# More copied tiles in a two-layer graph network: a second table, a third engine for its columns, and a narrower one-hot

## The chip, the core and the metric

The kernel runs on one core of a Trainium2 chip. A core has TensorE (PE), VectorE (DVE), ScalarE (ACT), GpSimd (POOL) and SyncE (SP), each with an instruction queue of its own that it works through in order; semaphores tie them together. The metric is the device time of one execution in microseconds, as the median of several runs. The lower the better.

## The reference

12,500 nodes have 128 features each, and 200,000 edges, sorted by their target `dst`, have 50 features each. Both layers add to `x` what they compute of its normalized form:

```python
h = relu(layernorm(x))
x = x + segment_sum(h[src], dst) @ W_rel.T + b_rel + h @ W_root.T
h = relu(layernorm(x))
w = silu(edge_attr_50 @ We1 + be1) @ We2 + be2
agg = segment_sum(h[src] * w, dst)
x = x + silu(agg @ Wn1 + bn1) @ Wn2 + bn2
```

All of it is f32.

## The kernel before

**Groups.** The edges are cut into tiles of 128 and groups of 8 tiles (`GT`), 196 groups a layer, the last with 3 tiles. Group g of both layers does the same: POOL gathers the source rows of a tile from DRAM into one of six buffers `hs` (`fetch`, line 250: one indirect DMA for a tile of 128 rows). DVE compares the targets with a row of numbers and so makes a one-hot `oh` of `W` = 128 nodes for each edge (`compare`, line 263). PE multiplies the rows with the one-hot, 8 matmuls into one PSUM window of 128 columns (`scatter`, line 376); since the edges are sorted, a group's targets lie in a window of few nodes. DVE adds the window to the sums in SBUF, `agg`, at an offset read from a register (`add`, line 394). In the second layer, PE and ACT make the edge weights for the group (`hidden`, `weigh`, lines 340, 343 and 353), and DVE adds the bias and multiplies (lines 361 and 365) ahead of the scatter.

**Copied tiles.** All of the normalized nodes lie transposed in SBUF, in `table`: a node is a column of 128 numbers. Some tiles are therefore not gathered by POOL, but put together from this table: the 128 source columns are copied one by one into a tile `hc`, at offsets that the engine reads into registers from a list, 16 at a time (`take`); DVE copies by an OR with zero on bytes (line 585), ACT by a copy (line 587). PE turns the tile (`turn`, line 612) and ACT places it into the last slot of its group's `hs` (`place`, line 618). `HELP` tells how many tiles are copied in how many groups, `HC` which columns of each tile DVE copies and which ACT. With `HELP = ((1, 1), (9, 10))`, one tile a group is copied in the first layer from group 30 on, and nine tiles in ten groups in the second from group 26 on: 160 + 147 tiles, each placed four groups (`HW`) after its copying. POOL issues the other 2819 gathers.

**First groups.** The table and the normalized nodes in DRAM, `h0_d`, are made beside the first groups of the first layer: `node_first` normalizes one batch of 512 nodes a group, stores it, turns it on PE, and ACT copies it into the table (line 449). Until group `FG` = 29 the groups gather from the raw `x`, and each tile is normalized after the gather (`norm`, two units a group). `push` runs a unit's second half after the first half of the next one. From FG on they gather from `h0_d`.

**Node steps.** When the last edge of a batch of 512 nodes is surely added, its node step runs: in the first layer `node_sum` (PE sums, DVE adds `x` and starts the statistics, ACT takes the deviation, DVE clears that part of `agg`), `node_norm`, `node_keep` and `node_store`, over four groups. The result h1 goes to DRAM, where the second layer gathers. For the second layer's table, each batch of h1 is loaded again from DRAM (`node_again`), turned and copied into `table` (`node_turn`) beside its first 26 groups.

**Order of the work.** It is written out by hand. The loop over groups records, for group g: the gathers of g + 1, the compare of g + 1, the add of g - 1, the scatter of g, then whatever `plan` has put beside g, then `spread`, which records this group's share of the column copies on DVE and ACT. `at` records a wait, `inc` an increment. Each engine's queue has this order and nothing else.

Of the kernel before, what the change touches and what calls it, by code (L numbers as in the profile page):

```python
# [10 lines left out]
F32 = mybir.dt.float32  # L11
# [12 lines left out]
W = 128  # L24
# [10 lines left out]
HELP = ((1, 1), (9, 10))  # L35
HC = (60, 56)
# [30 lines left out]
def helped(n_nodes, n_edges):  # L67

    ng = n_edges // GE
    nbt = len(last_groups(n_nodes, n_edges))
    layers = []
    for begin, (tiles, groups) in ((min(ng, nbt + FB) + 1, HELP[0]), (nbt + 1, HELP[1])):
        ends = (begin - 1 - -(i + 1) * groups // tiles for i in range(ng * tiles // groups))
        layers.append((begin, [(e + HW, e) for e in ends if e + HW < ng - 1]))
    return layers

# [12 lines left out]
def kernel(  # L92
# [41 lines left out]
    FG = min(NG, NBT + FB)  # L134
    helps = [
        (layer, h, e, begin, j)
        for layer, (begin, groups) in enumerate(helped(N, n_edges))
        for j, (h, e) in enumerate(groups)
    ]
    helped_groups = {(layer, h) for layer, h, *_ in helps}  # L140
# [17 lines left out]
    table = single([P, -(-N // P) * P], "table")  # L158
    agg = single([P, NW * WG], "agg")
    keep = table.rearrange("p (t d) -> p t d", d=D)  # L160
    table_b = table.bitcast(U8)
# [15 lines left out]
    with (  # L177
# [13 lines left out]
        hid = many(2, [P, GT * P], "hid")  # L191
        st, mv = many(2, [P, NB, 6], "st"), many(2, [P, NB, 2], "mv")
# [6 lines left out]
        help_i, = many(1, list(help_t.shape), "help_i", I32)  # L199
# [41 lines left out]
        def fetch(layer, g):  # L241
# [7 lines left out]
            for t in range(tiles_of[g] - ((layer, g) in helped_groups)):  # L249
                ins = G.indirect_dma_start(  # L250
                    out=hs[k % HB][:, t, :], out_offset=None,
                    in_=h1_d if layer else x if g < FG else h0_d,
                    in_offset=bass.IndirectOffsetOnAxis(
                        ap=src_sb[:, g * GT + t : g * GT + t + 1], axis=0
                    ),
                )
                done["hs", k] = inc(ins, f"hs{k % HB}", 16)
# [12 lines left out]
        def stats(xr, n, rows, st_, mv_, sd_, free):  # L270
# [7 lines left out]
            at(A, inc(ins, "dve"))  # L278
# [3 lines left out]
        def scales(n, rows, mv_, sd_, rs_, nm_, deviations):  # L282
            at(V, deviations)
# [50 lines left out]
        def hidden(g):  # L334
            n = tiles_of[g] * P
            at(T, done["ef", g // EG], done.get(("hid", g - 1)), done["const"])
            e = ef[g // EG % 2][:EF, g % EG * GE : (g % EG + 1) * GE]
# [4 lines left out]
            at(A, done["hp", g], done.get(("wp", g - 2)))  # L342
# [41 lines left out]
        def add(layer, g):  # L384
# [7 lines left out]
            at(V, done["ap", k], done.get(("add", k - 1)), done["agg"])  # L392
            window = agg[:, ds(firsts[k - g % GL][g % GL], W)]
# [51 lines left out]
        def node_table(b, turned):  # L445
# [3 lines left out]
            ins = A.copy(table[:, n0 : n0 + m], turned.rearrange("p t d -> p (t d)")[:, :m])  # L449
            done["table", b] = inc(ins, "act")  # L450

        def node_sum(b):

            n0, nt = batches[b]
            at(T, done.get(("keep", b - 1)), done["const"], done["ones"], done["table", b])
            T.matmul(op[:, :nt, :], ones_r, b_rel_r[:, :nt, :], start=True, stop=False)
            for layer_agg, w_sb in ((table, w_root_sb), (agg, w_rel_sb)):
                for t in range(nt):
                    s = n0 + t * P
                    ins = T.matmul(  # L460
                        op[:, t, :], layer_agg[:, s : s + P], w_sb,
                        start=False, stop=(layer_agg is agg and t == nt - 1),
                    )
                at(T, done["add", ready[b]])
            done["op", b] = inc(ins, "pe")
            at(V, done["op", b], done["xt", b])
            o = op[:, :nt, :]
            ins = V.tensor_add(o, o, xt[b % XB][:, :nt, :])  # L468
            done["dev", b] = stats(
                op, nt, P, stn[2], mvn[2], sdn[2], (inc(ins, "dve"), done.get(("h1", b - 1)))  # L470
            )
            ins = V.memset(agg[:, n0 : n0 + nt * P], 0.0)
            done["agg"] = inc(ins, "dve")

        def node_norm(b):
            n0, nt = batches[b]
            at(A, scales(nt, P, mvn[2], sdn[2], rsn[2], nmn[2], done["dev", b]))
            if b < 2:
                at(A, *(done["h0 out", b] for b in range(max(0, NBT - 3), NBT)))
            else:  # L480
                at(A, done["h1 out", b - 2], done["keep", b - 2])
# [20 lines left out]

        def node_again(b):

            i = b % 3
            at(S, done["h1 out", b], done.get(("turned again", b - 3)))
            if b < 3:
                at(S, *(done["h1 out", c] for c in range(max(0, NBT - 2), NBT)))
            done["h1 in", b] = node_dma(b, h0[i], h1_d, f"h1in{i}", True)

        def node_turn(b):

            n0, nt = batches[b]
            at(T, done["h1 in", b], done["b3"])
            for t in range(nt):
                ins = T.transpose(op[:, t, :], h0[b % 3][:, t, :], ident)  # L516
            done["turned", b] = done["turned again", b] = inc(ins, "pe")
            at(A, done["op", NBT - 1], *done.get("columns", ()))
            node_table(b, op)
            done["b3"] = done["table", b]  # L520

        def node_hidden(b):
# [3 lines left out]
            ins = T.matmul(b3[:, :m], wn1_sb, agg[:, n0 : n0 + m], start=True, stop=True)  # L526
# [31 lines left out]
        def chunks(layer, g, engine):  # L558

            first, last = (0, HC[layer]) if engine is V else (HC[layer], P)  # L560
# [5 lines left out]
        def take(engine, chunk):  # L566
# [3 lines left out]
            kind = mybir.EngineType.DVE if engine is V else mybir.EngineType.Activation  # L570
            _, places = nc.values_load_multi_w_load_instructions(  # L571
                help_at[i % P : i % P + 1, i // P, lo:hi], engines=[kind],
                min_val=TABLE, max_val=TABLE + 4 * (N - 1),
                skip_runtime_bounds_check_because="sources are nodes",
            )
            return chunk, places

        def put(engine, taken):

            (i, lo, hi), places = taken  # L580
            at(engine, done.get(("tile", i - 3)), *(done["table", b] for b in range(NBT)))
            for c, place_ in zip(range(lo, hi), places):
                to, column = hc_b[i % 3][:, 4 * c : 4 * c + 4], table_b[:, ds(place_ - TABLE, 4)]
# [6 lines left out]

        def spread(layer, g):
# [4 lines left out]
            for engine, rest in ((V, hooks), (A, list(chunks(layer, g, A)))):  # L596
                for chunk in rest or (chunks(layer, g, V) if engine is V and not layer else ()):
                    put(engine, take(engine, chunk))
            hooks.clear()

# [13 lines left out]
        def place(i, layer, h):  # L614
# [3 lines left out]
            done["hx", k] = done["placed", i] = inc(A.copy(hs[k % HB][:, GT - 1, :], bank), "act")  # L618
# [3 lines left out]
        with tc.tile_critical():  # L622
# [32 lines left out]
            done["agg"] = inc(A.copy(agg, zero.to_broadcast([P, NW * WG])), "act")  # L655
# [9 lines left out]
            ins = V.tensor_scalar(help_at, help_i, 4.0, float(TABLE), op0=ALU.mult, op1=ALU.add)  # L665
# [42 lines left out]

            for layer, parts in (
                (0, (node_sum, node_norm, node_keep, node_store)),  # L710
                (1, (node_hidden, node_out, node_out_store)),
            ):
                begin = 0 if layer else FG
                for b in range(NBT):
                    begin = max(begin, ready[b] + 1)
                    for i, part in enumerate(parts):
                        plan(layer, begin + i, lambda b=b, part=part: part(b))
                    begin += len(parts) - 1
            for b in range(min(XB, NBT)):
                plan(0, NBT + 1, lambda b=b: node_load(b))  # L720
            for b in range(NBT):
                plan(1, b - 1, lambda b=b: node_again(b))
                plan(1, b, lambda b=b: node_turn(b))
            for b in range(min(2, NBT)):
                plan(1, ready[0] - 1, lambda b=b: node_load(b, keep_d))
            for i, (layer, h, e, begin, j) in enumerate(helps):
# [6 lines left out]
                if not layer:  # L733
                    plan(0, e + 2, lambda i=i, h=h: place(i, 0, h))
# [240 lines left out]
```

## Time and profile before

| | |
|---|---|
| median of 3 runs | 3561.74 us (3557.4 to 3564.12) |
| the profiled execution | 3553.55 us, its span 3551.7 us |
| POOL busy | 2662.7 us (75%), 2819 gathers |
| ACT busy | 2620.0 us (74%), 21464 column copies |
| DVE busy | 2510.7 us (71%), 17832 column copies |
| PE busy | 2286.8 us (64%), weight loads 1833.0 us |
| first gather starts | 3.06 us |
| last gather ends | 3533.43 us |
| granted TensorE clock, mean | 0.753 |

How to read it: a row of the costliest groups names the line, the engine, the operation and its tiles, then the count, the busy time and the mean of one in ns, and behind the bar how long the engine sat idle just before such instructions and what ended most of that. "issue" is idle time in which the engine waited for nothing that the profile shows. A timeline row gives start and length in us. An f32 matmul stands as two records, each with a weight load (PEld).

### The profile page before, as it was taken

The numbers are of one execution on the slowest core, as the hardware profiler recorded it, in microseconds if no ns is written. First come the engines' busy times: TensorE is split into PE (matmuls) and PEld (weight loads), VectorE is DVE, ScalarE is ACT, GpSimd is POOL, SyncE is SP. The second block draws the span as 40 slices with busy tenths as digits, with TensorE's granted clock in tenths as the row PEclk, the third lists the DMA queues.
The fourth block names the chain that finished last, engine by engine and source line by source line (L and its number), as shares of the span: only waits on it lengthen the run. The fifth ranks groups of instructions, "written<-read, shape, count | busy, mean of one in ns | idle before, by whom it ended". The sixth has DMA issues, their size and how long they took to land.

```text
span 3551.7 us, 73201 instructions
## 1 busy us (share of the span) xinstructions
PE 2286.8 (64%) x11405; PEld 1833.0 (52%) x11405; DVE 2510.7 (71%) x20197; ACT 2620.0 (74%) x22584; POOL 2662.7 (75%) x2826
## 2 busy tenths in 40 slices
PE   3444455445454454455567778878888788888887
PEld 3443444444444444444456566656566566566565
DVE  5555777676766767776433378888888888888885
ACT  6554888788878878887511278987888789888984
POOL 7777777777777777777677777777777777777776
PEclk7566656666666667656678888898888888988988
DMA  4332322222222222222233333332332233333322
GB/s 123 106 96 74 83 69 63 63 66 69 63 63 68 66 63 66 69 61 60 84 105 105 95 82 86 88 85 79 87 89 83 81 87 90 84 83 86 87 82 62
DMA packets 201107, 284.08 MB, mean 80 GB/s; under 512 B 49305, under 2 KB 150260, under 8 KB 195620
## 3 DMA queue, kind: packets, MB, share of 16 engines
q0 software_dynamic: 90208, 184.93, 20.0%
q1 hardware_dynamic: 110214, 94.30, 8.7%
q14 instruction: 396, 3.24, 0.3%
q8 instruction: 93, 1.52, 0.2%
q10 hardware_dynamic: 196, 0.09, 0.0%
HBM read 253.52 MB, written 25.60 MB: 79 GB/s over the span
## 4 chain that ended last, share of the span: by engine, by line
POOL 59%; issue 20%; PE 9%; DVE 5%; DMA 5%; ACT 2%; DVEq 0%; ACTq 0%; POOLq 0%; SPq 0%
POOL hs L250 59%; DMA hs<-h_d,src_sb 5%; PE bank L376 4%; PE pair L353 2%; ACT hc L587 2%; DVE hc L585 2%; DVE hs L365 2%; PE pair L340 1%; DVE pair L361 1%; PE bank L460 0%; DVE oh L263 0%; PE bank L526 0%; DVEq L571 0%; DVE xt L545 0%; ACTq L571 0%
## 5 line engine op out<-in xcount | busy, mean ns | idle before, releaser
L250 POOL DMA_INDIRECT hs<-h_d,src_sb x2587 | 2442.5, 944 | 798.5 <-issue 776.6
L587 ACT COPY hc<-table 128x4 uint8 x21464 | 2135.3, 190 | 63.3 <-issue 52.1
L376 PE MATMUL bank<-oh,hs 128*128 128x128 f32 x6252 | 1214.2, 373 | 671.7 <-DVE hs L365 300.2
L376 PEld LDWEIGHTS bank<-oh,hs 128*128 128x128 f32 x6252 | 1127.2, 279 | 885.1 <-DVE hs L365 435.4
L585 DVE TENSOR_TENSOR hc<-table,bank 128x4 uint8<-128x4 uint8 x17832 | 1303.1, 150 | 282.6 <-issue 274.7
L263 DVE TENSOR_TENSOR oh<-bank,rel 128x1024 f32<-128x1024 f32 x392 | 475.0, 1212 | 0.1
L353 PE MATMUL pair<-we_sb,hid 128*128 128x128 f32 x3126 | 428.7, 296 | 3.4 <-DVE xt L488 3.4
L361 DVE TENSOR_TENSOR pair<-pair,be_sb 128x1024 f32<-128x1024 f32 x196 | 240.2, 1226 | 261.1 <-PE pair L353 260.8
L353 PEld LDWEIGHTS pair<-we_sb,hid 128*128 128x128 f32 x3126 | 418.5, 215 | 3.5 <-DVE xt L488 3.5
L340 PE MATMUL pair<-ef,we_sb 50*128 50x512 f32 (+1 forms) x782 | 409.3, 645 | 1.2 <-ACT hid L343 1.2
L365 DVE TENSOR_TENSOR hs<-pair,hs 128x1024 f32<-128x1024 f32 x196 | 239.4, 1221 | 163.5 <-DMA hs<-h_d,src_sb 151.8
L612 PE MATMUL pair<-ident,hc 128*128 128x128 f32 x160 | 64.1, 401 | 434.6 <-ACT hc L587 277.2
L343 ACT ACTIVATE hid<-pair,be_sb 128x1024 f32<-128x1024 f32 x196 | 216.9, 1107 | 106.8 <-PE pair L340 106.3
L250 POOL DMA_INDIRECT hs<-in_x,src_sb x232 | 219.0, 944 | 71.2 <-issue 70.4
L612 PEld LDWEIGHTS pair<-ident,hc 128*128 128x128 f32 x160 | 28.7, 180 | 460.1 <-issue 141.1
L340 PEld LDWEIGHTS pair<-ef,we_sb 50*128 50x128 f32 x782 | 135.0, 192 | 132.7 <-issue 120.2
L279 ACT ACTIVATE sdn<-mvn,eps 128x4 f32<-128x4 f32 (+1 forms) x50 | 14.5, 289 | 247.0 <-DVE mvn L277 247.0
L449 ACT COPY table<-bank 128x512 f32<-128x512 f32 (+1 forms) x25 | 14.4, 577 | 176.2 <-PE bank L516 176.2
L528 ACT ACTIVATE hid<-bank,bn_sb 128x512 f32<-128x512 f32 (+1 forms) x25 | 17.0, 678 | 153.9 <-PE bank L526 153.9
L274 DVE BATCH_NORM_STATS2 st<-hs 128x6 f32<-128x128 f32 x232 | 50.3, 279 | 111.2 <-DMA hs<-in_x,src_sb 111.2
L394 DVE TENSOR_TENSOR agg<-agg,bank 128x128 f32 x392 | 109.2, 279 | 27.0 <-PE bank L376 19.7
L468 DVE TENSOR_TENSOR bank<-bank,xt 128x512 f32<-128x512 f32 (+1 forms) x25 | 17.2, 688 | 149.4 <-PE bank L460 149.4
(68 smaller groups left out, 910.4 us busy)
## 6 DMA issues: line engine op xcount, KB each, us to landing
hs<-h_d,src_sb POOLq DMA_INDIRECT x2587
ef<-in_ef_t SPq DMA_DIRECT2D x98, 408.0 KB
xt<-in_x SPq DMA_DIRECT2D x48, 256.0 KB, 3.9
h_d<-h SPq DMA_DIRECT2D x48, 256.0 KB, 2.5
keep_d<-xt SPq DMA_DIRECT2D x24, 256.0 KB, 2.4
h<-h_d SPq DMA_DIRECT2D x24, 256.0 KB, 5.3
xt<-keep_d SPq DMA_DIRECT2D x24, 256.0 KB, 10.0
out_x<-xt SPq DMA_DIRECT2D x24, 256.0 KB, 2.7
```

Of the source, the lines that this page charges most:

```text
L250: ins = G.indirect_dma_start(out=hs[k % HB][:, t, :], out_offset=None, in_=h1_d if layer else x if g < FG else h0_d, in_offset=bass.Indire ...
L263: return V.tensor_tensor(oh[k % OB][:, :n, :], io.unsqueeze(1).to_broadcast([P, n, W]), rel[:, g, :n].unsqueeze(2).to_broadcast([P, n, W]) ...
L340: ins = T.matmul(hp_b[:, c : c + m], we1_sb, e[:, c : c + m], start=True, stop=True)
L343: ins = A.activation(hid[g % 2][:, :n], hp_b[:, :n], AF.Silu, bias=be1_sb)
L353: ins = T.matmul(wp[:, t, :], hid[g % 2][:, t * P : (t + 1) * P], we2_sb, start=True, stop=True)
L361: ins = V.tensor_add(w, w, be2_sb.unsqueeze(1).to_broadcast([P, n, D]))
L365: done["msg", g] = inc(V.tensor_mul(h, w, h), "dve")
L376: ins = T.matmul(ap[k % AB], hs[k % HB][:, t, :], oh[k % OB][:, t, :], start=(t == 0), stop=(t == tiles_of[g] - 1),)
L394: done["add", k] = inc(V.tensor_add(window, window, ap[k % AB]), "dve")
L585: ins = V.tensor_tensor(to, column, zero_b, ALU.bitwise_or)
L587: ins = A.copy(to, column)
L612: done["tile", i] = inc(T.transpose(bank, hc[i % 3], ident), "pe")
```

## The change

- **Copied tiles.** `HELP` becomes six tiles in five groups of the first layer and nineteen in twenty groups of the second. Where two tiles fall into one group, a `slot` tells them apart. They begin at group 18 in the first layer and at group 1 in the second: 206 + 179 tiles.
- **A third engine.** In the first layer, the last 12 of a tile's 128 columns are moved by PE: a matmul of the identity with one column of the table, into PSUM (`move`); in the next group ACT copies the piece into `hc` (`empty`). DVE copies columns 0 to 55 and ACT 56 to 115 in the first layer; 0 to 59 and 60 to 127 in the second. In the first layer one list of DVE's is now read ahead, after the compare (`hook`).
- **Tables sooner.** Two batches of nodes are normalized a group instead of one, so `FG` is 17 instead of 29.
- **Two tables.** `table` and `agg` become the two halves of one tile `both`. The first layer's table is the first half and its sums are the second; in the second layer it is the other way round. The second layer's table is made in the node step of the first: `node_turn` turns h1 from SBUF, and `node_send` copies it over the sums just used. `node_again`, with its loads from DRAM, is gone. The old table is cleared for the new sums by four copies on ACT (`clear`) beside groups 191 to 194, its last two batches by DVE.
- **Node steps.** The parts of a node step lie a group apart, over seven groups, and closer together in the last ones.
- **One-hot.** `W` is 80 instead of 128.

Cut to its core:

```diff
-W = 128
+W = 80
...
-HELP = ((1, 1), (9, 10))
-HC = (60, 56)
+HELP = ((6, 5), (19, 20))
+HC = ((56, 116), (60, 128))
...
-    for begin, (tiles, groups) in ((min(ng, nbt + FB) + 1, HELP[0]), (nbt + 1, HELP[1])):
-        ends = (begin - 1 - -(i + 1) * groups // tiles for i in range(ng * tiles // groups))
-        layers.append((begin, [(e + HW, e) for e in ends if e + HW < ng - 1]))
+    for begin, (tiles, groups) in ((min(ng, -(-nbt // 2) + FB) + 1, HELP[0]), (1, HELP[1])):
+        ends = [begin - 1 - -(i + 1) * groups // tiles for i in range(ng * tiles // groups)]
+        slots = [ends[:i].count(e) for i, e in enumerate(ends)]
+        layers.append((begin, [(e + HW, s, e) for s, e in zip(slots, ends) if e + HW < ng - 1]))
     return layers
+def help_places(n_nodes, n_edges):
+    places, begins, begin = [], [], 0
+    for _, groups in helped(n_nodes, n_edges):
+        begins.append(begin)
+        places += [(j % P, begin + j // P) for j in range(len(groups))]
+        begin += -(-max(len(groups), 1) // P)
+    return places, begins + [begin]
...
-    FG = min(NG, NBT + FB)
+    FG = min(NG, -(-NBT // 2) + FB)
...
-    table = single([P, -(-N // P) * P], "table")
-    agg = single([P, NW * WG], "agg")
-    keep = table.rearrange("p (t d) -> p t d", d=D)
-    table_b = table.bitcast(U8)
+    both = single([P, 2 * NW * WG], "both")
+    halves = both[:, : NW * WG], both[:, NW * WG :]
+    agg = halves[1]
+    keep = halves[0].rearrange("p (t d) -> p t d", d=D)
+    both_b = both.bitcast(U8)
...
-            for t in range(tiles_of[g] - ((layer, g) in helped_groups)):
+            for t in range(tiles_of[g] - helped_groups.count((layer, g))):
...
         def hidden(g):
...
+            if g < 2:
+                at(T, done.get(("emptied", done.get("moved"))))
...
-            window = agg[:, ds(firsts[k - g % GL][g % GL], W)]
+            window = halves[1 - layer][:, ds(firsts[k - g % GL][g % GL], W)]
...
-            at(T, done.get(("keep", b - 1)), done["const"], done["ones"], done["table", b])
+            at(T, done.get(("sent", b - 1)), done["const"], done["ones"], done["table", b])
             T.matmul(op[:, :nt, :], ones_r, b_rel_r[:, :nt, :], start=True, stop=False)
-            for layer_agg, w_sb in ((table, w_root_sb), (agg, w_rel_sb)):
+            for half, w_sb in zip(halves, (w_root_sb, w_rel_sb)):
                 for t in range(nt):
                     s = n0 + t * P
                     ins = T.matmul(
-                        op[:, t, :], layer_agg[:, s : s + P], w_sb,
-                        start=False, stop=(layer_agg is agg and t == nt - 1),
+                        op[:, t, :], half[:, s : s + P], w_sb,
+                        start=False, stop=(half is agg and t == nt - 1),
                     )
                 at(T, done["add", ready[b]])
             done["op", b] = inc(ins, "pe")
+
+        def node_moments(b):
+            n0, nt = batches[b]
             at(V, done["op", b], done["xt", b])
             o = op[:, :nt, :]
             ins = V.tensor_add(o, o, xt[b % XB][:, :nt, :])
-            done["dev", b] = stats(
-                op, nt, P, stn[2], mvn[2], sdn[2], (inc(ins, "dve"), done.get(("h1", b - 1)))
-            )
-            ins = V.memset(agg[:, n0 : n0 + nt * P], 0.0)
-            done["agg"] = inc(ins, "dve")
+            means[b] = moments(op, nt, P, stn[2], mvn[2], (inc(ins, "dve"), done.get(("h1", b - 1))))
+            if b >= cleared:
+                at(V, done["op", b], *done.get("columns", ()))
+                ins = V.memset(halves[0][:, n0 : n0 + WG], 0.0)
+                done["sums", 1].append(inc(ins, "dve"))
+
+        def clear(b0, b1):
+
+            at(A, done["op", b1 - 1], *done.get("columns", ()))
+            s0, s1 = b0 * WG, b1 * WG
+            ins = A.copy(halves[0][:, s0:s1], zero.to_broadcast([P, s1 - s0]))
+            done["sums", 1].append(inc(ins, "act"))
+
+        def node_deviations(b):
+            means[b] = deviations(batches[b][1], P, mvn[2], sdn[2], means[b])
+
+        def node_scales(b):
+            means[b] = scales(batches[b][1], P, mvn[2], sdn[2], rsn[2], nmn[2], means[b])
...
-        def node_again(b):
-            i = b % 3
-            at(S, done["h1 out", b], done.get(("turned again", b - 3)))
-            if b < 3:
-                at(S, *(done["h1 out", c] for c in range(max(0, NBT - 2), NBT)))
-            done["h1 in", b] = node_dma(b, h0[i], h1_d, f"h1in{i}", True)
         def node_turn(b):
             n0, nt = batches[b]
-            at(T, done["h1 in", b], done["b3"])
+            at(T, done["h1", b], done["keep", b])
             for t in range(nt):
-                ins = T.transpose(op[:, t, :], h0[b % 3][:, t, :], ident)
-            done["turned", b] = done["turned again", b] = inc(ins, "pe")
-            at(A, done["op", NBT - 1], *done.get("columns", ()))
-            node_table(b, op)
-            done["b3"] = done["table", b]
+                ins = T.transpose(op[:, t, :], h1[b % 2][:, t, :], ident)
+            done["h1 turned", b] = inc(ins, "pe")
+        def node_send(b):
+            n0, nt = batches[b]
+            at(A, done["h1 turned", b])
+            ins = A.copy(halves[1][:, n0 : n0 + nt * P], b3[:, : nt * P])
+            done["sent", b] = done["b3"] = inc(ins, "act")
...
+        moved = []
+        def move(taken):
+            (i, lo, hi), columns = taken
+            n = done["moved"] = done.get("moved", 0) + 1
+            bank = hp_b[:, n % 2 * WG :][:, : hi - lo]
+            at(T, done["checked"], done.get(("emptied", n - 2)), *(done["table", b] for b in range(NBT)))
+            for c, place_ in enumerate(columns):
+                column = both_b[:, ds(place_ - TABLE, 4)].bitcast(F32)
+                ins = T.matmul(bank[:, c : c + 1], ident, column, start=True, stop=True)
+            moved.append((n, i, lo, hi, bank, inc(ins, "pe")))
+        def empty():
+            for n, i, lo, hi, bank, full in moved:
+                at(A, full, done.get(("tile", i - 3)))
+                done["emptied", n] = inc(A.copy(hc[i % 3][:, lo:hi], bank), "act")
+                done["columns", i, False] = done["emptied", n]
+                done["columns"] = [done.get(("columns", i, kind)) for kind in (True, False)]
+            moved.clear()
         def spread(layer, g):
             for taken in hooked:
                 put(V, taken)
             hooked.clear()
             for engine, rest in ((V, hooks), (A, list(chunks(layer, g, A)))):
-                for chunk in rest or (chunks(layer, g, V) if engine is V and not layer else ()):
+                for chunk in rest:
                     put(engine, take(engine, chunk))
             hooks.clear()
+            for chunk in chunks(layer, g, T):
+                move(take(T, chunk))
...
-            done["hx", k] = done["placed", i] = inc(A.copy(hs[k % HB][:, GT - 1, :], bank), "act")
+            done["hx", k] = done["placed", i] = inc(A.copy(hs[k % HB][:, GT - 1 - slot, :], bank), "act")
...
+            cleared = NBT
             for layer, parts in (
-                (0, (node_sum, node_norm, node_keep, node_store)),
-                (1, (node_hidden, node_out, node_out_store)),
+                (0, (
+                    (0, node_sum), (1, node_moments), (2, node_deviations), (3, node_scales),
+                    (4, node_norm), (5, node_keep), (5, node_store), (5, node_turn), (6, node_send),
+                )),
+                (1, ((0, node_hidden), (1, node_out), (2, node_out_store))),
             ):
                 begin = 0 if layer else FG
                 for b in range(NBT):
                     begin = max(begin, ready[b] + 1)
-                    for i, part in enumerate(parts):
+                    if not layer and begin > NG - 6:
+                        cleared = min(cleared, b)
+                    for i, part in parts:
+                        if not layer and begin > NG - 9:
+                            i //= 3
                         plan(layer, begin + i, lambda b=b, part=part: part(b))
-                    begin += len(parts) - 1
+                    begin += i
+            for i in range(4):
+                b0, b1 = (cleared * j // 4 for j in (i, i + 1))
+                if b0 < b1:
+                    plan(0, NG - 5 + i, lambda b0=b0, b1=b1: clear(b0, b1))
             for b in range(min(XB, NBT)):
-                plan(0, NBT + 1, lambda b=b: node_load(b))
-            for b in range(NBT):
-                plan(1, b - 1, lambda b=b: node_again(b))
-                plan(1, b, lambda b=b: node_turn(b))
+                plan(0, -(-NBT // 2) + 1, lambda b=b: node_load(b))
...
-                plan(0, max(NG - 7, FG + 2), lambda g=g: hidden(g))
+                plan(0, max(NG - 4, FG + 2), lambda g=g: hidden(g))
...
+                        hooks.extend(chunks(0, g, V))
                         if g + 1 < NG:
                             compared = compare(0, g + 1)
+                            hook()
                             if not g:
                                 done["oh", 1] = inc(compared, "dve")
                         if g < FG:
+                            if 2 * g < NBT:
+                                push(node_first(2 * g))
                             for c in range(-(-tiles_of[g] // NB)):
                                 push(norm(g, c))
-                            push(node_first(g) if g < NBT else nothing)
+                            push(node_first(2 * g + 1) if 2 * g + 1 < NBT else nothing)
...
+                    empty()
                     for what in beside[layer].get(g, ()):
                         what()
                     spread(layer, g)
```

Left out are the list of columns, which `help_places` now lays out by layer and slot, and the names that follow from the two halves.

## The prediction

> **What bounds the kernel now.** I read the page first: busy shares and costliest groups.
>
> ```profile
> PE 2286.8 (64%) x11405; PEld 1833.0 (52%) x11405; DVE 2510.7 (71%) x20197; ACT 2620.0 (74%) x22584; POOL 2662.7 (75%) x2826
> ...
> L250 POOL DMA_INDIRECT hs<-h_d,src_sb x2587 | 2442.5, 944 | 798.5 <-issue 776.6
> L587 ACT COPY hc<-table 128x4 uint8 x21464 | 2135.3, 190 | 63.3 <-issue 52.1
> L376 PE MATMUL bank<-oh,hs 128*128 128x128 f32 x6252 | 1214.2, 373 | 671.7 <-DVE hs L365 300.2
> ...
> L585 DVE TENSOR_TENSOR hc<-table,bank 128x4 uint8<-128x4 uint8 x17832 | 1303.1, 150 | 282.6 <-issue 274.7
> L263 DVE TENSOR_TENSOR oh<-bank,rel 128x1024 f32<-128x1024 f32 x392 | 475.0, 1212 | 0.1
> ```
>
> Four engines stand between 64% and 75%, so shares decide nothing. The gathers of POOL are idle almost only for "issue". The view of POOL's waits says how evenly:
>
> ```profile
> POOL hs L250 <- issue: 847.0, 2779, 0.3
> POOL hs L250 <- DMA h_d<-h: 10.3, 1, 10.3
> ```
>
> No gap is longer than 0.3 us but one of 10.3 us. POOL is never late: it issues gather after gather and sets the time alone. From the timeline the first gather starts at 3.06 us and the last ends at 3533.43, so (3533.43 - 3.06 - 10) / 2819 = 1.2488 us a gather. The span is 3.06 + 2819 x 1.2488 + 10 + 18.3 (from the last gather's end to the end) = 3551.7. The 10 us lie between the layers.
>
> The question is then whether the engines that copy columns keep up. The timelines of DVE, ACT and PE in the first layer, where a group (7 gathers) lasts 8.74 us on POOL:
>
> ```profile
> 904.47 1.19 DVE L585 TENSOR_TENSOR hc<-table,bank 128x4 uint8<-128x4 uint8 x16 [0.35 <-issue]
> 906.17 1.19 DVE L585 TENSOR_TENSOR hc<-table,bank 128x4 uint8<-128x4 uint8 x16 [0.52 <-issue]
> 907.63 0.91 DVE L585 TENSOR_TENSOR hc<-table,bank 128x4 uint8<-128x4 uint8 x12 [0.26 <-issue]
> 908.46 1.21 DVE L263 TENSOR_TENSOR oh<-bank,rel 128x1024 f32<-128x1024 f32 x1
> ```
>
> ```profile
> 900.97 6.87 ACT L587 COPY hc<-table 128x4 uint8 x68
> 907.74 0.25 ACT L618 COPY hs<-pair 128x128 f32<-128x128 f32 x1
> ```
>
> ```profile
> 904.85 3.78 PE L376 MATMUL bank<-oh,hs 128*128 128x128 f32 x16 [2.63 <-DMA hs<-h_d,src_sb]
> 908.60 0.48 PE L612 MATMUL pair<-ident,hc 128*128 128x128 f32 x1
> ```
>
> ACT takes 6.77 us for 68 columns (907.74 - 900.97), 0.0996 each; the lists of columns that it reads between cost nothing there. DVE takes 0.0735 a column and some 0.43 us more for each list of 16 that it reads (275 us of issue over about 640 lists). PE's 16 records (8 f32 matmuls) take 3.78 us; in the second layer, where PE is busier, the same line takes 2.05:
>
> ```profile
> 2713.66 2.05 PE L376 MATMUL bank<-oh,hs 128*128 128x128 f32 x16 [0.56 <-DVE hs L365]
> 2715.55 1.95 PE L353 MATMUL pair<-we_sb,hid 128*128 128x128 f32 x16
> ```
>
> The granted clock agrees: 0.64 in the first layer's stretches, 0.83 to 0.90 in the second's.
>
> **The change part by part.**
>
> **Gathers removed.** The rule in `helped` gives 160 + 147 copied tiles before and 206 + 179 after. 78 gathers fewer: 78 x 1.2488 = 97.4 us. This is on the path. A group of the first layer now lasts (8 - 1.2) x 1.2488 = 8.49 us on POOL, one of the second (8 - 0.95) x 1.2488 = 8.80. All helpers must fit into these.
>
> **ACT, first layer, per group.** 1.2 x 60 = 72 columns x 0.0996 = 7.17; placing 1.2 tiles at 0.155 (from the start of L618 to the next copy) = 0.19; emptying two PSUM pieces, 0.1 to 0.2 each = 0.3; node step (deviation 0.29, four norms 1.5, copy of the second table 0.585) / 8 groups = 0.3; issue gaps 52 us / 307 groups = 0.17, perhaps double, as lists are now as short as 4. Sum 8.1 to 8.5, taken 8.3 of 8.49. It fits by 2%.
>
> **DVE, first layer.** 67.2 columns x 0.0735 = 4.94; 4.8 lists, one read under the compare, 3.8 x 0.43 = 1.63; compare of 640 instead of 1024 elements, 1.13 to about 0.73 by proportion; add 0.28 to some 0.17; node work 2.95 / 8 = 0.37. Sum 7.8 of 8.49.
>
> **PE, first layer.** 14.4 columns a group by a matmul of one column against `ident`, each with a register instruction ahead of it in the built program. No row shows such a matmul. The page "TensorE: Matmul & The Clock Gate" of the Trainium skill (section on LDWEIGHTS) speaks against it: a weight load costs the stationary's columns / 1.2 ns, however few columns move, so 107 ns for `ident`. An f32 matmul is two records, so by the page 0.21 us a column, an estimate, and 3.1 us a group. The trace's nearest full-speed row, L353 with 16 loads of 128 columns, gives 1.95 / 16 = 0.122 a record, 0.244 a column, 3.5 a group. That is the floor, the trace's number taken; below nothing it cannot go, since no PE work is removed. The ceiling is the slow record (3.78 / 16 = 0.236, twice) with the register instruction in series (two adds of L394 in sequence stand 0.20 us apart at the end of the trace, against 0.04 for an ordinary wait: 0.16): 0.63 a column, 9.1 a group. I take 0.30: a PE this full should run as in the second layer, and reads its registers while the scatter still runs. With scatter 2.05 to 3.0, tile turns 0.33 and node step 0.5 (3.34 for the sums, 0.6 for the turns, over 8), PE needs 7.2 to 8.2, taken 7.7. By the same page narrowing the one-hot to 80 does not shorten the scatter, whose stationary keeps 128 columns; by proportion to moving columns it would be 1.3. I count no gain.
>
> **New waits.** ACT's emptying waits for PE's piece of the group before; behind it stand ACT's placing and all its columns. PE's move waits for ACT's emptying of two pieces ago; behind it stands the next scatter. PE's tile turn waits for columns of ACT and DVE, as before. With ACT at 8.3 and PE at 7.7 the ring closes inside 8.49; six `hs` buffers let POOL run about four groups (34 us) ahead, so a single late group costs nothing. Only an average above 8.49 counts: each 0.1 us is 0.1 x 172 groups (18 to 189) = 17 us.
>
> **Tables sooner.** Two node batches a group instead of one: four units a group instead of three. A unit is 0.2 + 1.63 us on ACT, so 4 x 1.9 + 2 x 0.56 = 8.7 of the 9.99 us of eight gathers. Hidden under POOL; ACT starts 13 us late (zeroing `agg`, 10.86) and recovers 1.3 a group, four groups before FG = 17. POOL's wait for the stored h0 should stay absent, as it is now. SP issues the same loads and stores at twice the rate, some 2 us of issue a group. If the cover fails, the lateness shows as a POOL wait before group 17: 0 to 15 us, taken 0.
>
> **Node steps a group apart, second table.** This takes ACT's waits for `mvn` (247 us over 25 batches) and DVE's for the sum (149) out of the queues. POOL did not wait for them, so 0 by itself, but with ACT at 8.3 of 8.49 waits of 10 us a batch (1.2 a group) would no longer be covered. Removed from layer two's start: 24 loads of 256 KB on SP, 98 transposes and 25 copies (0.585); the last two now lie in the first layer and are counted above. Clearing the old table on ACT, 10.86 x 23 x 512 / 12800 = 10 us in four parts, falls after the last copied columns.
>
> **Between the layers.** POOL's 10.3 us wait for the last stored h1 has the same chain (scatter, sum, norm, store). The sum now also waits for ACT's copy of the batch before. 8 to 18 us, taken 10.
>
> **Second layer.** ACT 0.95 x 68 x 0.0996 = 6.4, plus hidden 1.11, placing and node 0.25: 7.8 of 8.80. DVE 57 x 0.0735 = 4.2, plus 0.73, 0.17, 1.23, 1.22 and gaps 0.5: 8.1. PE as before. It fits, and from group 1 on instead of 26.
>
> **Sum.** 3.06 + 2741 x 1.2488 + 10 + 18.3 = 3454.3 us span. The profiled execution is 1.85 us longer than its span (3553.55) and lies 8.2 under the median of the runs: 3454.3 + 1.85 + 8.2 = 3464. I add 6 for stalls in the groups that carry a node step, an estimate: 3470.
>
> **The rivals.**
> - **Helpers at the edge.** ACT comes out at 8.5 to 9.0 with PE's answers: +2 to +88 us. For it: ACT's margin is 2% and three in-order queues now wait for each other each group. Against it: the removed node waits. Middle 8.7: 0.21 x 172 = 36, 3506.
> - **PE becomes the bound (the other side).** In the move of the first layer PE keeps the pace of its slow rows and the register instructions stand in series. A group of 8.49 + 97.4 / 172 = 9.06 us eats the gain. With 3.7 to 4.8 us of other PE work (scatter, turns, node step, lists read) that is 0.30 to 0.37 a column, so it decides at about 0.35. At 0.38 with 4.2 the group is 9.67: +203 us, 3667. For it: the slow scatters and the 0.64 clock. Against it: the second layer's clock under a full PE.
> - **It does nothing.** Freed POOL time comes back as POOL waits of the same sum, 9.06 a group, 3562. Only a chance meeting of costs does this.
>
> **How the numbers follow.** POOL keeps the bound: 0.53, own range 3450 to 3490. Edge: 0.26, 3466 to 3550. PE bound: 0.17, from 3555 up. No change: 0.04. The first two are faster, 0.79; same (within 0.2%, 7 us, about what measurement can tell) 0.04; slower 0.17. Range 3450 to 3575: it leaves out the long end of the PE case, some 0.14, and little below.
>
> **What would show it.** Right: 2741 gathers, POOL's waits all issue but one near 10 us, groups of 8.49 us in the first layer, ACT near 97% there and PE's granted clock up to 0.8. Wrong: POOL waits for L402 (the scatter) through the first layer; one-column matmuls above 0.35 us apart; ACT idle before the emptying copies (L650).

## The result, and the profile after

The changed kernel takes 3831.01 us (median of 4, 3825.52 to 3835.02) against 3561.46 before (median of 4): a ratio of 1.0757 (95% interval 1.0737 to 1.0777), 270 us slower. The profiled execution took 3835.02 us, its span 3833.5.

From the page of the kernel after, its busy shares and the groups that answer to those shown of before (columns as there):

```profile
PE 3479.4 (91%) x16427; PEld 3056.8 (80%) x16427; DVE 2629.9 (69%) x24379; ACT 2948.8 (77%) x25957; POOL 2594.7 (68%) x2748
...
L267 POOL DMA_INDIRECT hs<-h_d,src_sb x2605 | 2464.6, 946 | 1167.7 <-issue 740.5
L629 ACT COPY hc<-both 128x4 uint8 x24532 | 2437.4, 190 | 142.2 <-issue 115.1
L627 DVE TENSOR_TENSOR hc<-both,bank 128x4 uint8<-128x4 uint8 x22276 | 1632.5, 150 | 494.5 <-issue 270.0
...
L402 PE MATMUL bank<-oh,hs 128*128 128x80 f32 x6252 | 1245.5, 382 | 235.4 <-DVE hs L391 170.3
...
L643 PE MATMUL pair<-both,ident 128*128 x4944 | 1030.2, 342 | 0.0
```

POOL has its 2741 gathers (2605 + 136) and is busy 68 us less than before, but its idle time has grown. PE has gone from 64% to 91%, 1030 us of it in the new column matmuls (L643). The view of POOL's waits names who holds it (total, times, longest):

```profile
POOL hs L267 <- issue: 781.7, 2555, 2.5
POOL hs L267 <- PE pair L678: 266.7, 114, 8.8
POOL hs L267 <- PE bank L402: 135.9, 55, 30.7
POOL hs L267 <- DMA h_d<-h: 20.0, 1, 20.0
```

Of the first row almost all is the 0.3 us that lies between any two gathers; the next two are waits for a free `hs` buffer, hence for PE: by the program the gather waits for a scatter (L402), and the tile turn (L678) that the first of them names runs right behind it. The timeline of PE in the first layer, 900 to 913 us:

```profile
901.94 3.68 PE L402 MATMUL bank<-oh,hs 128*128 128x80 f32 x16
905.41 0.42 PE L678 MATMUL pair<-ident,hc 128*128 128x128 f32 x1
905.63 6.83 PE L643 MATMUL pair<-both,ident 128*128 x32
912.31 3.68 PE L402 MATMUL bank<-oh,hs 128*128 128x80 f32 x16
```

There is no idle time in it. The scatter of 80 columns takes 3.68 us, where 128 columns took 3.78. The 16 columns of the move take 912.31 - 905.63 = 6.68 us, 0.418 each. And the granted clock is low all the while. I cut both traces into one stretch of each layer; the columns are span, then busy us and count for PE, weight loads, DVE, ACT and POOL, then the granted clock, DMA share and GB/s. Before:

```profile
352.00:1584.00 1232.00, 612.38 (x2740) 538.04 (x2740) 879.76 (x9014) 1006.53 (x9865) 931.19 (x988) 0.64 0.25 67
2112.00:3344.00 1232.00, 1011.09 (x5343) 759.81 (x5342) 1026.48 (x7573) 1063.15 (x9313) 931.18 (x988) 0.87 0.31 85
```

After:

```profile
352.00:1584.00 1232.00, 1232.00 (x5776) 1207.28 (x5777) 742.52 (x8384) 930.80 (x8993) 770.08 (x816) 0.51 0.21 55
2112.00:3344.00 1232.00, 1078.59 (x5163) 823.74 (x5163) 1001.52 (x8202) 1020.60 (x8873) 918.49 (x973) 0.79 0.30 83
```

In the first layer PE is busy for all 1232 us, at a granted clock of 0.51, lower than the 0.64 of a PE that was half idle. (Below, a clock near 0.5 is called half, one of 0.8 and more open.) The chain of work that ended last lies on PE for the whole of this stretch, 55.7% of it in the column matmuls and 33.8% in the scatter. 816 gathers at 6.8 a group are 120 groups, 10.27 us each instead of the 8.49 that POOL needs. In the second layer, where the change adds next to nothing to PE (179 tiles to turn instead of 147) and narrows its scatter, the clock has fallen from 0.87 to 0.79.

Where the time went: for every gap of POOL above 0.45 us in the timeline I take what it has over the usual 0.3 us, and add these up in three parts: the first layer until 100 us before the first gather of the second, those 100 us (the seam), and all after. Below, these sums are called POOL's excess, and a gather with such a gap is a held one.

| | first layer | seam | second layer |
|---|---|---|---|
| before | 0.5 | 10.0 | 0 |
| after | 271.1 | 62.1 | 41.4 |

From the last gather's end to the end of the span it is 28.0 us instead of 18.3. With POOL's 3423 us for 2741 gathers and 3 at the start these sum to 3829 of 3833.5.

### The profile page after: what moved, and what is told of

It is laid out like the page before. It is cut to its first block, busy times and chain, and to the rows that moved or that the text cites. A ratio compares the mean times of both kernels' runs of the same rounds, so it can differ in the third digit from the quotient of the medians.

```text
span 3833.5 us, 94075 instructions
## 1 busy us (share of the span) xinstructions
PE 3479.4 (91%) x16427; PEld 3056.8 (80%) x16427; DVE 2629.9 (69%) x24379; ACT 2948.8 (77%) x25957; POOL 2594.7 (68%) x2748
## 4 chain that ended last, share of the span: by engine, by line
PE 69%; DVE 16%; POOL 5%; ACT 5%; issue 3%; DVEq 1%; ACTq 0%; DMA 0%; POOLq 0%; SPq 0%
PE pair L643 26%; PE bank L402 25%; PE pair L379 8%; DVE hc L627 6%; POOL hs L267 5%; DVE hs L391 4%; DVE pair L387 4%; ACT hc L629 4%; PE pair L366 3%; PE bank L488 2%; PE bank L484 1%; PE pair L678 1%; DVEq L612 1%; DVE oh L280 1%; PE bank L577 1%
## 5 line engine op out<-in xcount | busy, mean ns | idle before, releaser
L629 ACT COPY hc<-both 128x4 uint8 x24532 | 2437.4, 190 | 142.2 <-issue 115.1
L627 DVE TENSOR_TENSOR hc<-both,bank 128x4 uint8<-128x4 uint8 x22276 | 1632.5, 150 | 494.5 <-issue 270.0
L402 PEld LDWEIGHTS bank<-oh,hs 128*128 128x128 f32 x6252 | 1179.2, 290 | 416.8 <-DVE hs L391 299.6
L402 PE MATMUL bank<-oh,hs 128*128 128x80 f32 x6252 | 1245.5, 382 | 235.4 <-DVE hs L391 170.3
L643 PEld LDWEIGHTS pair<-both,ident 128*128 128x128 f32 x4944 | 1051.2, 326 | 0.0
L643 PE MATMUL pair<-both,ident 128*128 x4944 | 1030.2, 342 | 0.0
L379 PE MATMUL pair<-we_sb,hid 128*128 128x128 f32 x3126 | 538.5, 344 | 0.0
L379 PEld LDWEIGHTS pair<-we_sb,hid 128*128 128x128 f32 x3126 | 515.7, 258 | 0.0
L280 DVE TENSOR_TENSOR oh<-bank,rel 128x640 f32<-128x640 f32 x392 | 318.7, 813 | 0.2
L420 DVE TENSOR_TENSOR both<-both,bank 128x80 f32 x392 | 91.7, 234 | 192.9 <-PE bank L402 170.9
L267 POOL DMA_INDIRECT hs<-in_x,src_sb x136 | 128.9, 948 | 42.0 <-issue 41.2
L678 PE MATMUL bank<-ident,hc 128*128 128x128 f32 x179 | 56.9, 318 | 41.2 <-DVE xt L584 24.4
L678 PEld LDWEIGHTS bank<-ident,hc 128*128 128x128 f32 x179 | 29.0, 162 | 64.0 <-ACT hid L567 34.4
```

Source lines behind the costliest of these rows:

```text
L267: ins = G.indirect_dma_start(out=hs[k % HB][:, t, :], out_offset=None, in_=h1_d if layer else x if g < FG else h0_d, in_offset=bass.Indire ...
L280: return V.tensor_tensor(oh[k % OB][:, :n, :], io.unsqueeze(1).to_broadcast([P, n, W]), rel[:, g, :n].unsqueeze(2).to_broadcast([P, n, W]) ...
L379: ins = T.matmul(wp[:, t, :], hid[g % 2][:, t * P : (t + 1) * P], we2_sb, start=True, stop=True)
L402: ins = T.matmul(ap[k % AB], hs[k % HB][:, t, :], oh[k % OB][:, t, :], start=(t == 0), stop=(t == tiles_of[g] - 1),)
L627: ins = V.tensor_tensor(to, column, zero_b, ALU.bitwise_or)
L629: ins = A.copy(to, column)
```

## The experiments

Ratios are to the kernel before, run alongside on the same chip: 3559.63 us for the first four runs, 3556.22 for the next four, 3555.65 for the last three.

**No columns on PE, one-hot of 80.**

```diff
-HC = ((56, 116), (60, 128))
+HC = ((60, 128), (60, 128))
```

> The changed kernel with PE's 12 columns of each first-layer tile given back: DVE 60, ACT 68, PE none. Theory (PE's one-column matmuls, 0.427 us a column at half clock, set the pace of the first layer): PE drops below 8 us a group, ACT with 81.6 columns x 0.0996 + 0.5 = 8.6 to 8.9 us a group becomes the bound; the first layer loses some 250 us, 3520 to 3580 us in all. Rival (six tiles in five groups make a ring of in-order queues that is too tight, whoever copies): little gained, above 3750 us.

Measured: 3579.84 us, ratio 1.0045 (1.0030 to 1.0060), at the upper end of the theory's range. POOL's excess gaps are 16.0, 52.6 and 54.5 us: the first layer is cured, the seam and the second layer are not. PE is now busy for 54% of the first stretch, and its clock is as low as before:

```profile
352.00:1584.00 1232.00, 668.56 (x2783) 588.87 (x2781) 917.23 (x10509) 1183.22 (x11659) 922.25 (x976) 0.51 0.25 65
```

So the PE columns cost the first layer its 250 us, but something else that the change brought costs about 100 in the rest.

**The one-hot at 128 again, all else as changed.**

```diff
-W = 80
+W = 128
```

> The changed kernel with the one-hot at 128 nodes again. Theory A (PE's scatter is set by its weight loads of 128 columns; narrowing only makes PE count as less busy, and its clock in the second layer fell from 0.88 to 0.78): the first layer stays within 10 us, the second layer's clock returns to 0.85 or more and its 40 us of POOL waits go: 3780 to 3800 us. Theory B (the narrower one-hot shortens PE's scatter): the first layer gets longer by 0.3 us or more a group, 50 us, 3880 us or more.

Measured: 3483.27 us, ratio 0.9795 (0.9774 to 0.9816). Neither theory had this: one constant turns 7.6% slower into 2% faster. The second layer does what theory A says; the first, which both had unchanged or longer, is 270 us shorter. The same two stretches of this run, and PE's timeline in the first layer:

```profile
352.00:1584.00 1232.00, 1211.49 (x6987) 1173.08 (x6986) 951.83 (x10107) 1105.76 (x10859) 931.23 (x987) 0.66 0.26 66
2112.00:3344.00 1232.00, 1025.05 (x5384) 771.41 (x5384) 1098.98 (x8549) 1064.40 (x9302) 931.18 (x988) 0.87 0.31 85
```

```profile
906.57 2.78 PE L643 MATMUL pair<-both,ident 128*128 x24
909.20 3.00 PE L402 MATMUL bank<-oh,hs 128*128 128x128 f32 x16
912.00 0.42 PE L678 MATMUL pair<-ident,hc 128*128 128x128 f32 x1
912.50 6.98 PE L643 MATMUL pair<-both,ident 128*128 x32
919.35 3.76 PE L402 MATMUL bank<-oh,hs 128*128 128x128 f32 x16
```

The same column matmul now runs in two speeds: 24 records in 2.63 us from start to the next start, 0.22 a column, and a little later 32 records in 6.85, 0.43 a column. The wider scatter, which moves 1.6 times as many columns, takes 3.76 us when slow against 3.68: next to nothing more. What it buys is a clock that opens part of the time, and POOL is not held in either layer (0.6 and 0 us of excess; 31.6 at the seam).

**The kernel before with the one-hot at 80, nothing else.**

```diff
-W = 128
+W = 80
```

> The kernel before with the one-hot at 80 nodes and nothing else. If POOL alone bounds it: 3555 to 3568 us, no change. If the narrower one-hot lowers PE's clock in the second layer enough to hold POOL up: clock there below 0.83 instead of 0.88, POOL waits of 10 to 40 us, 3570 to 3600 us.

Measured: 3574.55 us, ratio 1.0041 (1.0026 to 1.0056), with POOL's excess at 0.7, 11.9 and 10.6 us; another 10 us lie after the last gather (28.5 us instead of 18.3). The second theory holds, at the low end of its 10 to 40 us of waits:

```profile
352.00:1584.00 1232.00, 635.14 (x2739) 567.07 (x2739) 821.22 (x9013) 1004.91 (x9855) 931.48 (x986) 0.54 0.26 67
2112.00:3344.00 1232.00, 1107.53 (x5213) 852.16 (x5214) 943.86 (x7410) 1041.31 (x9064) 931.68 (x986) 0.77 0.31 84
```

Less to move, and PE is busier: 1107.5 instead of 1011.1 us in the second stretch. The rows of the weights' matmul, an instruction that was not touched, tell why; in the kernel before, and with the one-hot at 80:

```profile
L353 PE MATMUL pair<-we_sb,hid 128*128 128x128 f32 x3126 | 428.7, 296 | 3.4 <-DVE xt L488 3.4
```

```profile
L353 PE MATMUL pair<-we_sb,hid 128*128 128x128 f32 x3126 | 545.5, 347 | 3.4 <-DVE xt L488 3.4
```

Beside the narrow scatter this neighbour is slower, by 117 us in sum.

**Each PE column streamed 32 times, one-hot of 80.** The moving operand is the column broadcast, and one of the outputs is used. Cut to the matmul:

```diff
...
-ins = T.matmul(bank[:, c : c + 1], ident, column, start=True, stop=True)
+ins = T.matmul(bank[:, c, :], ident, column.to_broadcast([P, 32]), start=True, stop=True)
...
```

> The changed kernel with each of PE's columns streamed 32 times (a broadcast moving operand of 32, of whose outputs one is used). Theory A (PE's clock stays at 0.50 through the first layer, though PE is never idle, because one-column matmuls hardly count as array work): the granted clock there rises above 0.7, a column falls from 0.427 towards 0.25 us, a group from 10.6 to below 9 us, 3500 to 3620 us. Theory B (the clock is held down by something else, or a column is bound by its issue): clock 0.50 and time within 20 us of 3831, or longer by the 31 further columns, up to 3900 us.

Measured: 3822.77 us, ratio 1.0750 (1.0725 to 1.0774), clock 0.52 in the first layer, and 0.418 us a column as before (6.68 us for 16 in the timeline). Theory A failed at this width; 31 more columns per matmul cost nothing that shows.

**Each PE column streamed 128 times, one-hot of 80.** Column c is written over places c to c + 127, and the next overwrites all but the first. Cut to the matmul:

```diff
...
-ins = T.matmul(bank[:, c : c + 1], ident, column, start=True, stop=True)
+ins = T.matmul(wide[:, c : c + P], ident, column.to_broadcast([P, P]), start=True, stop=True)
```

> The changed kernel (one-hot of 80) with each of PE's columns streamed 128 times into overlapping places, of which one output stays. Theory A (the clock opens when the moving operands keep the array busy for most of a stretch; at 80 of 128 columns in the slow state they do not, nor did 32): the granted clock of the first layer rises above 0.6, a column falls below 0.35 us, 3480 to 3650 us, though the column itself streams 128 times as much. Theory B (it is the scatter alone that matters, or the widths of one-hot on DVE): a column takes 0.47 us at half clock, 3870 to 3950 us.

Measured: 3525.11 us, ratio 0.9902 (0.9872 to 0.9932). Theory A: the same result, 128 times as much streamed, 306 us less. PE's timeline and the stretch of the first layer:

```profile
907.20 2.01 PE L402 MATMUL bank<-oh,hs 128*128 128x80 f32 x16 [1.24 <-DMA hs<-h_d,src_sb]
909.05 0.27 PE L679 MATMUL pair<-ident,hc 128*128 128x128 f32 x1
909.16 2.84 PE L644 MATMUL pair<-both,ident 128*128 x24
```

```profile
352.00:1584.00 1232.00, 1008.20 (x7091) 946.50 (x7091) 910.40 (x10276) 1118.04 (x11032) 931.52 (x986) 0.86 0.26 66
```

The clock is 0.86; a column takes 2.84 / 12 = 0.237 us and the scatter of 80 columns 2.01. PE waits for gathers again. The second layer, which has no PE columns, keeps its clock of 0.79 and 54.4 us of POOL's gaps.

**One-hot of 128 without PE columns.** The two edits of the first two experiments together.

> One-hot of 128 and no PE columns (DVE 60, ACT 68 of each first-layer tile). If PE's share of the columns is worth something once its clock is open: ACT at 8.6 to 8.9 us a group is the bound, 3500 to 3540 us, slower than with PE's share (3483). If not: 3483 or less.

Measured: 3532.36 us, ratio 0.9933 (0.9916 to 0.9949). In the range: beside the wide one-hot PE's share is worth 49 us. POOL's excess is 36.9 us in the first layer; 961 gathers in the stretch of 1232 us are 8.72 us a group, with ACT busy for 94% of it.

**Scatter of 128, all the rest of 80.** Columns 80 to 127 of the one-hot tiles are zeros, written once; DVE compares and adds 80. Cut to its core:

```diff
-        oh = many(OB, [P, GT, W], "oh")
+        oh = many(OB, [P, GT, P], "oh")
...
-                oh[k % OB][:, :n, :],
+                oh[k % OB][:, :n, :W],
...
-            done["add", k] = inc(V.tensor_add(window, window, ap[k % AB]), "dve")
+            done["add", k] = inc(V.tensor_add(window, window, ap[k % AB][:, :W]), "dve")
...
```

> The changed kernel with PE's scatter streaming 128 columns of the one-hot tile (columns 80 to 127 are zeros, written once at the start), while DVE compares and adds only 80. Theory A (PE's moving width alone makes the difference between 80 and 128): first-layer clock 0.64 or more, 3465 to 3490 us, at or a little under the 3483 of the one-hot of 128, since DVE saves 0.5 us a group. Theory B (something else of the one-hot's width, on DVE or in the windows): near 3831 us.

Measured: 3480.22 us, ratio 0.9788 (0.9752 to 0.9824); clock 0.65 and 0.88, no held gathers in either layer. Theory A: it is PE's moving width, and nothing of DVE's or of the windows. DVE's saving shows in its busy time (900.58 against 951.83 us in the first stretch) and not in the time.

**One-hot of 104.**

> The changed kernel with the one-hot at 104 nodes. [...] If the clock opens by a threshold between: either as at 128 (3470 to 3500 us) or as at 80 (3800 to 3835 us); a smooth dependence would give about 3640 us.

Measured: 3710.02 us, ratio 1.0411 (1.0370 to 1.0453). None of the three: it is between, nearer to 80. Cut into stretches of 176 us, the first layer alternates, with clocks of 0.57, 0.52, 0.57, 0.52, 0.52, 0.52, 0.52 and 0.56 from 352 us on; the three above 0.52 have 125 to 136 gathers, the others 114 to 120. The second layer has 0.84. So one width that switches the whole layer from half to open is not what these runs show; how the clock decides within a stretch stays open.

**Both streams 128 wide.** The scatter of 128 with DVE at 80, and the columns streamed 128 times.

> The changed kernel with both of PE's small streams widened: the scatter streams 128 columns (DVE still compares and adds 80) and each of PE's columns is streamed 128 times, one output of which stays. If the array's streaming share opens the clock: 0.85 or more in both layers, PE with slack in the first layer, POOL waiting only between the layers: 3460 to 3478 us, at or under the 3480 of the widened scatter alone. If the extra streaming costs more than the clock gives: 3480 to 3500.

Measured: 3468.67 us, ratio 0.9747 (0.9734 to 0.9761), the fastest of all together with the last one. The first theory:

```profile
352.00:1584.00 1232.00, 969.02 (x7101) 912.21 (x7099) 913.19 (x10294) 1119.57 (x11028) 931.18 (x988) 0.90 0.25 66
2112.00:3344.00 1232.00, 1021.78 (x5389) 766.11 (x5388) 1043.79 (x8558) 1068.64 (x9362) 931.26 (x987) 0.87 0.31 85
```

POOL's excess is 0.6, 16.5 and 0 us. All that is left over the sum of the gathers is the seam and 24.8 us after the last gather.

**4 columns on PE instead of 12, one-hot of 80.**

```diff
-HC = ((56, 116), (60, 128))
+HC = ((60, 124), (60, 128))
```

> The changed kernel (one-hot of 80) with 4 columns of a first-layer tile on PE instead of 12 (DVE 60, ACT 64). Clock 0.50 as before, but PE's sum at that clock is 1.2 x 4 x 0.427 = 2.05 plus 3.5 for the scatter, 0.5 for turns and 0.9 for node steps, 7 us a group against POOL's 8.49: PE no longer sets the pace, ACT takes 76.8 x 0.0996 + 1.0 = 8.6. 3490 to 3560 us. If not PE's sum but the ring of waits between PE and ACT were the cost: above 3600 us.

Measured: 3579.56 us, ratio 1.0067 (1.0050 to 1.0084). It missed the range by 20 us, but not in the first layer: there POOL's excess is 17.8 us at a clock of 0.51, so at half clock a PE with a third of the columns no longer sets the pace, and the ring of waits is not the cost. The miss is the seam (51.4) and the second layer (51.5), which the expectation left out.

**Both streams wide, five tiles in four groups.** HELP = ((5, 4), (19, 20)), HC = ((56, 112), (60, 128)).

> As with both streams widened, and five tiles in four groups instead of six in five (215 tiles in the first layer, 9 gathers fewer), with 16 columns a tile on PE and 56 on each of DVE and ACT. 9 x 1.249 = 11 us less if ACT (70 columns, 8.0 us) and PE (20 x 0.25 = 5.0 plus 3.2) stay under the 8.43 us of a group: 3450 to 3470 us. If PE's or DVE's queue is then the bound: 3480 to 3530 us.

Measured: 3468.98 us, ratio 0.9753 (0.9740 to 0.9766), at the upper end of the first range. No held gathers in the layers (0.6 and 0), clock 0.95 in the first. The 11 us of the 9 gathers are gone again at the seam: 34.6 us of excess instead of 16.5.

## Why the prediction was wrong

**Gathers and the bound before: right.** POOL issues 2741 gathers at its old pace wherever PE lets it. With both streams wide the last one ends at 3442.6 us; 3.06 + 2741 x 1.2488 + 16.5 is 3442.5.

**PE in the first layer: the step that failed.** The prediction took 0.30 us a column and 2.05 to 3.0 for the scatter, since "a PE this full should run as in the second layer". Measured: 0.418 a column and 3.47 from the scatter's start to the next start. With 0.26 for turns and 0.8 for node steps (5.6 us of sums from 1936.8 us on and 0.85 of turns, over 8 groups) PE's sum is 14.4 x 0.418 + 4.5 = 10.5 us a group, against 10.27 counted and 7.7 predicted. The bounds of a column held (0.244 to 0.63); the value between was chosen by a rule that failed. PE was fuller than before, and its clock lower; nor is being full what opens it: PE was 54% busy at 0.51 without its columns, 100% at 0.51 with them, and 79% at 0.90 with both streams wide. The rival on the other side had half of the mechanism right: PE kept its slow pace, but no register instruction shows in series, since a column (0.418) takes no more than two records of the scatter beside it (2 x 3.47 / 16 = 0.434), without the 0.16 on top. It decided at 0.35 and was priced at 0.38: 203 us, where the first layer lost 271.

The signs that the prediction had named for being wrong came: POOL waits for PE through the first layer, columns 0.418 us apart, and ACT idle before the emptying copies:

```profile
L650 ACT COPY hc<-pair 128x4 f32<-128x4 f32 (+2 forms) x343 | 54.3, 161 | 333.2 <-PE pair L643 332.6
```

**The one-hot: "I count no gain" hid a loss.** That narrowing does not shorten the scatter was right (3.68 against 3.78 us). But the prediction put the edit at nothing, and gave no bound for a loss. Undoing it alone takes 348 us from the changed kernel (3831.01 to 3483.27). The loss is not in the scatter; it is that the matmuls beside it stay slow (0.418 us a column throughout, against 0.22 in part of the time beside the wide one). It turned the PE columns of the first layer from covered to binding, and in the second layer took the clock from 0.87 to 0.79, worth 41 us of POOL's gaps, and part of the seam. The loss in the first layer needs both parts of the change: giving the PE columns back cures it too (16 us of excess), and so does widening them (3525.11).

**The page on weight loads.** The page "TensorE: Matmul & The Clock Gate" of the Trainium skill (section on LDWEIGHTS) led to the estimate of 0.21 us a column; the prediction's floor from the trace was 0.244. At an open clock a column, load and matmul together, measures 0.22 to 0.24, between the two, and at the half clock 0.42. Times the clock that is nearly the same (0.418 x 0.51 = 0.213 and 0.237 x 0.86 = 0.204), so a price fixed in ns could not tell whether PE would fit.

**ACT and DVE: right.** With PE out of the way they fit: ACT is busy for 91% and DVE for 74% of the first stretch, and no gather is held. Without PE's share the group takes 8.72 us beside the wide one-hot, for 8.6 to 8.9 expected.

**Tables sooner: right.** No POOL wait falls before group 17; the first above 2 us comes at 426 us.

**Seam: too small.** 10 us taken, 8 to 18 as bounds. Measured 62 in the changed kernel. The prediction looked only at the wait for the last stored h1, which is 20.0 us there. Another 30.7 us fall earlier, at 1937 us: in the last eight groups of a layer the program lets the gathers run only three groups ahead of the scatter (`LB`) instead of six, so a scatter that is several groups behind is waited for there. With both streams wide it is not behind, and only the wait for h1 is left: an excess of 16.5, inside the bounds.

**Second layer: a miss of 41 us.** "PE as before" left out the clock.

The number itself, 3470 us, is what the change gives where the clock rises: 3468.67 with both streams wide (0.90 in the first layer), 3480.22 with the wide scatter alone (0.65). That the first comes within 2 us is in part luck: its seam and its end take 6.5 us more each than was reckoned, while the 6 us for stalls (0.6 measured) and the 8.2 between the profiled run and the median (3469.12 and 3468.67) did not come. That the clock is what was missing is shown by the widths; what exactly it counts was not measured.

## What to carry to other kernels

Before work is added to PE or taken from it, look at the granted clock of the stretch, and ask what the edit does to it: here a busy PE of narrow moving operands ran at half speed, and a useless widening of a stream made the kernel faster. When a cost is put at nothing, bound it on the side of loss too. And undo each constant of a compound change by itself: here the loss of the first layer needed two of them, undoing either one cured it, and the one that looked harmless was worth 348 us.

## What was not expected of the hardware

PE can be busy without a gap and stay at a granted clock of 0.50 to 0.54 (in stretches of 44 us, from 264 to 1936 us here), when its moving operands are 1 and 80 columns wide against weight loads of 128. A column streamed 1 or 32 times takes 0.42 us there, and 128 times 0.237, since the clock opens to 0.86. For scatters of 80, 104 and 128 columns beside the same column matmuls the clock of the first layer was 0.51, 0.53 and 0.66, and of the second 0.79, 0.84 and 0.87.
